# GpSimd's two additions of the output projection's first product, put behind the powers of the layer norms

## The chip, the cores and the metric

The kernel runs on one core of a Trainium2 chip. The metric is the device time of one execution in microseconds (us): before the change the median of six runs is 3116.72 us (3115.21 to 3117.72). The engines of the core work side by side, each through its own list of instructions in a fixed order: TensorE (PE, with its weight loads shown as PEld), VectorE (DVE), ScalarE (ACT), GpSimd (POOL), and SyncE (SP), which here issues the DMAs. An instruction that needs another engine's result waits for a semaphore, and everything behind it on its own engine waits too.

## The reference

For each of 64 batch elements (256 nodes, 512 features) two layers with residual and layer norm are computed in float32:

```python
x = layernorm(x + deg*(x @ Wi.T + b) + adj @ (x @ Wj.T))       # layer 0, a graph layer
q, k, v = (x @ W.T + b  for the three weights)                 # layer 1: attention, 8 heads of 64
attn = softmax(where(adj == 0, -inf, q @ k.T / 8))
x = layernorm(x + (attn @ v) @ Wo.T + bo)
```

`layernorm` subtracts the row's mean and divides by the root of its variance plus 1e-5.

## The kernel before

**Pairs of elements.** The loop at line 982 takes two batch elements per turn `g` (b1 and b2); 32 pairs make the whole, and 31 of them go through the loop. In the turn for pair `g` the attention of pair `g` is computed, and woven into it layer 0 of pair `g+1`, then the output projection of `g` and the projections q, k and v of `g+1`. A turn takes 95.97 us in the trace (the start of the same instruction in successive turns: 1010.83 and 1106.78 us).

**Seven products in place of eight.** Every product with a 512 by 512 weight is made of 2 by 2 blocks by a Strassen-Winograd scheme: seven block products (`pair_steps`, line 646, `block_product`, line 636; eight matmuls each). The left factors are the blocks A11, A12 (of b1), A21, A22 (of b2) and four sums S1 to S4 of them (`left_steps`, line 476, on DVE). For the output projection the blocks lie in `aoT`, which holds the attention's output, and the sums in `oS`. Each product is accumulated in a PSUM bank (tag `mm`, three banks) and then taken out by a `use` function. The order in which the seven run is that of `second_late`: A11, A12, A22, S2, S1, S3, S4.

**The output projection, `o_steps` (line 733).** Its results are added in place to `xh`, which holds the residual. `use1` copies the first product (A11) out of PSUM to a tile `u1` with ACT (line 743), and then GpSimd adds `u1` to one block of b1 (line 746, 128x512) and to both halves of b2 (line 747, 128x1024). The other `use` functions add on DVE (line 740).

**Attention's division.** The sums of the exponentials of a pair of heads come out of four matmuls (`den`); DVE inverts them (line 882), GpSimd adds the inverses to a running total (line 883), DMAs spread them over the partitions (`spread`, line 890), and `multiply` (line 841) multiplies a block of `aoT` by `spread` on GpSimd (line 844). The last division of a turn, `divide_two(g, w + 1)`, concerns block A22 of `aoT`. Its `multiply` therefore has to be over before the sums S1 to S4 are made and before A22 is used by the third product of the output projection.

**The layer norm.** `norm_stats` (line 451) takes mean and variance of 128 rows on DVE, adds 1e-5 (`ve`, line 457), keeps the negated mean (`below`, line 459), and GpSimd raises `ve` to the power -0.5 (`rstd`, line 461). `norm_apply` (line 464) then does two ACT instructions (`shift`, line 466, and `xh`, line 467). In layer 0, `neighbours` multiplies by the graph on TensorE, `take(1)` and `take(0)` add the result to `xh` (line 575) and call `norm_stats`, `give(1)` and `give(0)` call `norm_apply`, and `send_h` writes the rows to DRAM (line 599), from where they come back for a transposition.

**What sets the order.** A planner puts the instructions of each engine in a fixed order when the kernel is built. It goes by its own estimate of when each is ready. `in_order` pins an instruction behind the instruction that the program text issued just before it on the same engine; a pinned one may not overtake that, and an instruction that isn't pinned may be placed earlier. All matmuls are pinned, so TensorE follows the text. `multiply`, `add_bias` and `add_output_bias` on GpSimd are pinned, lines 461, 746 and 747 are not. In the trace of before, GpSimd runs lines 746 and 747 ahead of the two powers.

The place of the change is the end of a turn (lines 1007 to 1010). TensorE's list there is, after the den matmuls of `divide_two`: the first product of the output projection `o[0]` (A11), `neighbours`, `q[0]`, `o[1]` (A12), `k[0]`, `q[1]`, `k[1]`, and then `o[2:6]`, which begin with A22 and S2. `k[1]` accumulates in the bank of `k[0]`, and so it has to wait until ACT has copied `k[0]` out of it (line 711, through `biased`, with the bias `bk`). The copies of q and k are not pinned. The ACT instructions of the norms, lines 466 and 467, are.

The weights' factors come by DMA from SyncE, `next_factor` (line 445), eight tiles ahead.

Of the kernel before, what the change touches and what calls it, by code (L numbers as in the profile page):

```python
# [12 lines left out]
ALU = mybir.AluOpType  # L13
# [3 lines left out]
P = 128  # L17
# [207 lines left out]
def unshifted_path(ctx, tc, flag, x, adj, wiT, wjT, b0, wqT, bq, wkT, bk, wvT, bv, woT, bo, out):  # L225
# [16 lines left out]
    nc = tc.nc  # L242
    B, N, D = x.shape
    NT = N // P
# [5 lines left out]
    H = D // 2  # L250
# [31 lines left out]
    def in_order(ins):  # L282

        tc.keep_in_program_order(ins)
# [44 lines left out]
    mhalf = const.tile([P, 1], F32, name="mhalf")  # L329
# [118 lines left out]
        return f  # L448


    def norm_stats(t, order=anywhere):
        st = small.tile([P, 6], F32, tag="st", name="st")
        order(nc.vector.bn_stats(st, t))
        mv = small.tile([P, 2], F32, tag="mv", name="mv")
        nc.vector.bn_aggr(mv, st)
        ve = small.tile([P, 1], F32, tag="ve", name="ve")
        nc.vector.tensor_scalar(ve, mv[:, 1:2], EPS, None, ALU.add)
        below = small.tile([P, 1], F32, tag="below", name="below")
        order(nc.vector.tensor_scalar(below, mv[:, 0:1], -1.0, None, ALU.mult))  # L459
        rstd = small.tile([P, 1], F32, tag="rstd", name="rstd")  # L460
        nc.gpsimd.tensor_tensor(rstd, ve, mhalf, ALU.pow)  # L461
        return below, rstd

    def norm_apply(t, below, rstd, order=anywhere):
# [37 lines left out]
    def l0_steps(b):  # L502
        banks, k = {}, {}

        def product(name, left, n, first):
            if first:
                banks[name] = bank("po")
            for c in range(2):
                matmul(banks[name], left[:, c, :], w0[:, n, c, :], start=(first and c == 0),
                                 stop=(c == 1), skip_group_check=True)  # L510

        def raw(t, h):
            return xT[b][:, 2 * h:2 * h + 2, t * P:(t + 1) * P]

        def keeper(name):
            k[name] = p3.tile([P, D], F32, tag="lu", name=name)
            return k[name]

        def add_scaled(t, src):
            nc.vector.scalar_tensor_tensor(xh[b][:, t, :], src, deg[:, t:t + 1], xh[b][:, t, :],  # L520
                                           ALU.mult, ALU.add)

        def split(t):
            nc.scalar.copy(k["hi"][:, t, :], k["mj"][:, t, :])
            nc.gpsimd.tensor_tensor(k["lo"][:, t, :], k["mj"][:, t, :], k["hi"][:, t, :].bitcast(F32),
                                    ALU.subtract)

        def step1():
            product("x", raw(0, 0), B11, True)
            nc.scalar.copy(keeper("u1"), banks["x"])  # L530

        def step2():
            product("w", raw(1, 1), T4, True)
            add_scaled(1, banks["w"])

        def step3():
            product("x", raw(0, 1), B21, False)
            add_scaled(0, banks["x"])

        def step4():  # L540
            product("y", xS[b]["S2"], T2, True)
            nc.vector.tensor_add(keeper("u2"), banks["y"], k["u1"])

        def step5():
            product("z", xS[b]["S1"], T1, True)
            k["mj"] = p1.tile([P, NT, D], F32, tag="mj", name="mj")
            nc.scalar.copy(k["mj"][:, 1, :], banks["z"])  # L547

        def step6():
            product("y", xS[b]["S3"], T3, False)  # L550
            nc.vector.tensor_add(keeper("u3"), banks["y"], k["u1"])
            nc.gpsimd.tensor_tensor(k["mj"][:, 1, :], k["mj"][:, 1, :], k["u3"], ALU.add)

            k["hi"] = p1.tile([P, NT, D], F32R, tag="hi", name="hi")
            k["lo"] = p1.tile([P, NT, D], F32R, tag="lo", name="lo")
            split(1)
            add_scaled(1, k["u3"])

        def step7():
            product("z", xS[b]["S4"], B22, False)  # L560
            nc.vector.tensor_add(k["mj"][:, 0, :], banks["z"], k["u2"])
            split(0)

        stats = {}

        def neighbours():
            k["pa"] = score_banks("pa")
            for i in (1, 0):
                for n, (j, part) in enumerate((j, part) for j in (1, 0) for part in ("hi", "lo")):
                    matmul(k["pa"][:, i, :], graph[:, j, i * P:(i + 1) * P], k[part][:, j, :],  # L570
                           start=(n == 0), stop=(n == 2 * NT - 1))

        def take(t):
            r = xh[b][:, t, :]
            in_order(nc.vector.tensor_add(r, k["pa"][:, t, :], r))
            stats[t] = norm_stats(r, in_order)

        def give(t):
            norm_apply(xh[b][:, t, :], *stats[t], in_order)


        return [step1, step2, step3, step4, step5, step6, step7, neighbours, lambda: take(1), lambda: take(0),
                lambda: give(1), lambda: send_h(b, 1), lambda: give(0), lambda: send_h(b, 0)]

# [83 lines left out]
    def second_late(steps):  # L668
        return [steps[0], steps[2], steps[1], *steps[3:]]
# [63 lines left out]
    def o_steps(g):  # L733
        b1, b2 = NB * g, NB * g + 1

        def place(i, j):
            return xh[NB * g + i][:, :, j * H:(j + 1) * H]

        def add_to(dst, src):
            nc.vector.tensor_add(dst, src, dst)  # L740

        def use1(bank, k, new):
            nc.scalar.copy(new("u1"), bank["x"])

            o = xh[b2].rearrange("p t (j o) -> p t j o", j=2)
            nc.gpsimd.tensor_tensor(place(0, 1), place(0, 1), k["u1"], ALU.add)
            nc.gpsimd.tensor_tensor(o, o, k["u1"].unsqueeze(2).to_broadcast([P, NT, 2, H]), ALU.add)

        def use2(bank, k, new):
            add_to(place(1, 0), bank["w"])  # L750

        def use3(bank, k, new):
            add_to(place(0, 0), bank["x"])

        def use4(bank, k, new):
            add_to(place(0, 1), bank["y"])

        def use5(bank, k, new):
            add_to(place(1, 1), bank["z"])

        def use6(bank, k, new):
            o = xh[b2].rearrange("p t (j o) -> p t j o", j=2)
            add_to(o, bank["y"].unsqueeze(2).to_broadcast([P, NT, 2, H]))

        def use7(bank, k, new):
            add_to(place(0, 1), bank["z"])

        steps = pair_steps(lambda: oS[g], False, (use1, use2, use3, use4, use5, use6, use7))
        return second_late(steps)

    def finish_steps(g):

# [136 lines left out]
    def run(steps):  # L909
        for s in steps:  # L910
            s()
# [7 lines left out]
    for g in range(-1, NG - 1):  # L919
        o, q, k, v = (order_of(name) for name in ("wo", "wq", "wk", "wv"))  # L920
# [18 lines left out]
    p, q = l0_steps(0), l0_steps(1)  # L939
# [18 lines left out]
    o = second_late(qk_steps(0, qT, "qT", bq_sb, bqd, True))  # L958
# [23 lines left out]
    for g in range(NG - 1):  # L982
        load_x(NB * (g + 2))
        load_x(NB * (g + 2) + 1)
        work = layer0(g + 1)
        run(work[0])
        for w in range(2, NB * NC, 2):
            values(g, w - 2)
            values(g, w - 1)
            multiply()  # L990
            divide_two(g, w - 1)
            scores(g, w)()
            if w == 4:
                run(work[2])
            later = scores(g, w + 1)
            later()
            run(work[w // 2 if w < 4 else w // 2 + 1])
        w = NB * NC - 2
        values(g, w)
        values(g, w + 1)  # L1000
        multiply()
        o = o_steps(g)
        q = second_late(qk_steps(g + 1, qT, "qT", bq_sb, bqd))
        k = second_late(qk_steps(g + 1, kT, "kT", bk_sb, bkd, True))
        v = second_late(v_steps(g + 1, True))
        neighbours, take1, take0, give1, send1, give0, send0 = work[SLOTS + 1]
        divide_two(g, w + 1)
        run([o[0], neighbours, take1, take0, q[0], give1, send1, o[1], give0, send0, multiply,
             *left_steps(oS[g], in_order), k[0], q[1], k[1]])
        run(o[2:6] + work[SLOTS + 2] + [v[0], o[6], v[1]])  # L1010
        end = finish_steps(g)
        k = with_output_bias(g + 1, k)[2:]
        run(q[2:5] + end[:1] + q[5:6] + end[1:2] + q[6:7] + end[2:3] + k[:1] + end[3:4] + k[1:] + end[4:] + v[2:3])
        turn_x(NB * (g + 2))
        sum_x(NB * (g + 2))
        if g + 2 < NG:
            add_bias(NB * (g + 2))
        run(v[3:5])
        run([scores(g + 1, 0), scores(g + 1, 1)])
        run(v[5:])  # L1020
# [93 lines left out]
```

## Time and profile before

| | |
|---|---|
| median of six runs | 3116.72 us |
| profiled execution, time | 3118.53 us |
| profiled execution, span from the first to the last instruction | 3116.7 us |
| granted TensorE clock, mean | 0.999 |
| PE busy | 3073.6 us (99%), 14598 matmuls |
| DVE busy | 2149.0 us (69%) |
| POOL busy | 1521.0 us (49%) |
| ACT busy | 1008.2 us (32%) |
| line 746 on POOL, 128x512 | 31 times, 1271 ns each |
| line 747 on POOL, 128x1024 | 31 times, 2359 ns each |
| line 461 on POOL, 128x1 | 256 times, 553 ns each |
| line 844 on POOL, 128x512 | 127 times, 1280 ns each |

Times in the trace are counted from the first instruction. A row of the timeline gives the start, the duration, the engine, the line, the operation, the tiles written and read, and how many instructions in a row were merged; in brackets stands how long the engine had been idle before it, and what ended that. "Busy" isn't the same as working at full rate: matmuls are pipelined, and the starts of matmuls that follow each other say more than their durations. All matmuls carry line 290, which is the helper that issues them, so they are told apart by their tiles: `st<-factor,aoT` and `st<-factor,oS` are the output projection, `st<-hT,factor` are q and k.

### The profile page before, as it was taken

How to read it: one execution, taken by the hardware profiler on the slowest of the kernel's cores; microseconds unless marked ns; L12 is line 12 of the kernel's file. 1: busy time of each engine (PE TensorE's matmuls, PEld its weight loads, DVE VectorE, ACT ScalarE, POOL GpSimd, SP SyncE). 2: the span in 40 equal slices, each digit the busy share in tenths (PEclk: the TensorE clock that was granted, in tenths of full speed). 3: DMA queues.
4: the chain of work that ended last, by engine and by line, in shares of the span. 5: the costliest groups of instructions: out<-in, count | busy, mean ns of one | idle time of the engine just before them, and what ended most of it. 6: DMA issues, size and time to landing. Idle time of an engine off the chain costs nothing. (4 is left out here: it accounts for less than half of the span.)

```text
span 3116.7 us, 42777 instructions
## 1 busy us (share of the span) xinstructions
PE 3073.6 (99%) x14598; PEld 2118.5 (68%) x14598; DVE 2149.0 (69%) x3234; ACT 1008.2 (32%) x1925; POOL 1521.0 (49%) x1255
## 2 busy tenths in 40 slices
PE   7999999999999999999999999999999999999998
PEld 4667766677666777666776667766677766677665
DVE  6766676766677666676667676667766667767665
ACT  2332333323333333333233333333333333323332
POOL 2544545544545445464454544455544546445453
PEclk9999999999999999999999999999999999999999
DMA  7355534455444554445553445544455444555333
GB/s 247 122 149 157 166 118 133 131 157 164 141 123 125 156 167 148 119 129 153 158 164 117 126 142 157 165 136 125 127 154 169 141 123 128 154 162 162 115 109 99
DMA packets 410395, 447.28 MB, mean 144 GB/s; under 512 B 40896, under 2 KB 300224, under 8 KB 409792
## 3 DMA queue, kind: packets, MB, share of 16 engines
q1 hardware_dynamic: 410176, 444.50, 47.7%
q8 instruction: 120, 1.97, 0.3%
q14 instruction: 99, 0.81, 0.1%
HBM read 340.79 MB, written 70.25 MB: 132 GB/s over the span
## 5 line engine op out<-in xcount | busy, mean ns | idle before, releaser
L461 POOL TENSOR_TENSOR rstd<-ve,mhalf 128x1 f32<-128x1 f32 x256 | 140.5, 553 | 722.3 <-DVE below L459 722.3
L812 POOL TENSOR_TENSOR pk<-pe 128x512 f32<-128x512 f32 x256 | 322.3, 1275 | 340.7 <-ACT pe L809 340.7
L290 PE MATMUL po<-w,xS 128*128 128x512 f32 x1024 | 470.5, 602 | 6.1 <-ACT mj L547 5.6
L290 PE MATMUL st<-hS,factor 128*128 128x256 f32 x2048 | 452.7, 379 | 1.2 <-DVE u L685 1.2
L290 PEld LDWEIGHTS st<-hS,factor 128*128 128x128 f32 x2048 | 388.2, 190 | 55.3 <-DVE u L685 1.6
L809 ACT ACTIVATE pe<-pe 128x1024 f32<-128x1024 f32 x256 | 270.8, 1058 | 379.2 <-DVE pe L805 379.2
L290 PE MATMUL st<-hT,factor 128*128 128x256 f32 x1536 | 360.7, 381 | 9.0 <-ACT u L711 8.3
L290 PE MATMUL po<-w,xT 128*128 128x512 f32 x768 | 354.4, 604 | 14.6 <-DVE xS L479 9.3
L290 PEld LDWEIGHTS po<-w,xS 128*128 128x128 f32 x1024 | 187.0, 190 | 252.8 <-issue 191.4
L290 PEld LDWEIGHTS st<-hT,factor 128*128 128x128 f32 x1536 | 289.0, 190 | 61.5 <-ACT u L711 20.7
L805 DVE TENSOR_TENSOR pe<-ps,maskT 128x1024 f32<-128x1024 f32 x256 | 297.7, 1194 | 35.2 <-PE ps L290 35.2
L882 DVE RECIPROCAL rden<-den 128x256 f32<-128x256 f32 x127 | 222.8, 1754 | 73.9 <-PE den L290 68.4
L290 PEld LDWEIGHTS po<-w,xT 128*128 128x128 f32 x768 | 144.4, 192 | 182.9 <-issue 163.6
L290 PE MATMUL ps<-qT,kT 64*128 64x256 f32 x2048 | 264.9, 392 | 0.0
L883 POOL TENSOR_TENSOR rtot<-rtot,rden 128x256 f32<-128x256 f32 x127 | 92.7, 730 | 330.4 <-DVE rden L882 330.4
L290 PE MATMUL pav<-pe,v_sb 128*64 128x256 f32 x2048 | 250.1, 386 | 1.9 <-ACT pe L809 1.8
L740 DVE TENSOR_TENSOR xh<-st,xh 128x512 f32<-128x512 f32 x186 | 144.5, 777 | 147.8 <-PE st L290 147.7
L290 PEld LDWEIGHTS pav<-pe,v_sb 128*64 128x64 f32 x2048 | 135.2, 136 | 154.1 <-issue 72.0
L290 PEld LDWEIGHTS ps<-qT,kT 64*128 64x128 f32 x2048 | 184.3, 186 | 78.2 <-issue 51.3
L290 PE MATMUL st<-factor,hS 128*128 128x256 f32 x1024 | 234.8, 382 | 0.0
L290 PE MATMUL st<-factor,oS 128*128 128x256 f32 x992 | 224.2, 379 | 0.0
L290 PEld LDWEIGHTS st<-factor,hS 128*128 128x128 f32 x1024 | 191.9, 190 | 35.4 <-issue 10.6
(115 smaller groups left out, 4657.8 us busy)
## 6 DMA issues: line engine op xcount, KB each, us to landing
xB<-in_x_dram SPq DMA_DIRECT2D x256, 128.0 KB, 3.7
xh<-in_x_dram SPq DMA_DIRECT2D x64, 512.0 KB, 4.1
factor<-wq SPq DMA_DIRECT2D x128, 256.0 KB, 4.4
factor<-wk SPq DMA_DIRECT2D x128, 256.0 KB, 2.6
factor<-wv SPq DMA_DIRECT2D x128, 256.0 KB, 2.6
spread<-rden SPq DMA_DIRECT2D x1016, 32.0 KB, 1.9
factor<-wo SPq DMA_DIRECT2D x124, 256.0 KB, 3.0
h_cols<-xh SPq DMA_DIRECT2D x124, 256.0 KB, 2.5
```

The source lines that it names most:

```text
L290: in_order(nc.tensor.matmul(*args, **kw))
L461: nc.gpsimd.tensor_tensor(rstd, ve, mhalf, ALU.pow)
L740: nc.vector.tensor_add(dst, src, dst)
L805: nc.vector.tensor_add(pe.rearrange("p j t q -> p j (t q)"), ps.rearrange("p j t q -> p j (t q)"), maskT.rearrange("p t q -> p (t q)").uns ...
L809: in_order(nc.scalar.activation(flat, flat, AF.Exp, scale=QSCALE, accum_out=etot[:, NB * g + i, pr:pr + 1]))
L812: nc.gpsimd.tensor_tensor(pk, pe[:, :, 0, :], pe[:, :, 1, :], ALU.add)
L882: nc.vector.reciprocal(rden, den)
L883: nc.gpsimd.tensor_tensor(rtot, rtot, rden, ALU.add)
```

## The change

`norm_stats` gets a second argument, with which the power on GpSimd can be pinned; `take` in layer 0 gives it, so the powers of layer 0's norms are pinned behind what the text issued before them on GpSimd. The powers of the last norms (`finish_steps`) stay free. In `o_steps` the two GpSimd additions leave `use1` and become a step of their own, `add_first`, the eighth of the list (`o[7]`), and they are pinned. In the run of a turn's end that step stands behind `take0`. As `multiply` is pinned too, GpSimd's order at that place is fixed by the text: power, power, line 746, line 747, and then the multiplication of line 844.

```diff
-    def norm_stats(t, order=anywhere):
+    def norm_stats(t, order=anywhere, power_order=anywhere):
...
-        nc.gpsimd.tensor_tensor(rstd, ve, mhalf, ALU.pow)
+        power_order(nc.gpsimd.tensor_tensor(rstd, ve, mhalf, ALU.pow))
         return below, rstd
...
         def take(t):
             r = xh[b][:, t, :]
             in_order(nc.vector.tensor_add(r, k["pa"][:, t, :], r))
-            stats[t] = norm_stats(r, in_order)
+            stats[t] = norm_stats(r, in_order, in_order)
...
+        kept = []
+
         def use1(bank, k, new):
             nc.scalar.copy(new("u1"), bank["x"])
+            kept.append(k["u1"])
+
+        def add_first():
 
             o = xh[b2].rearrange("p t (j o) -> p t j o", j=2)
-            nc.gpsimd.tensor_tensor(place(0, 1), place(0, 1), k["u1"], ALU.add)
-            nc.gpsimd.tensor_tensor(o, o, k["u1"].unsqueeze(2).to_broadcast([P, NT, 2, H]), ALU.add)
+            in_order(nc.gpsimd.tensor_tensor(place(0, 1), place(0, 1), kept[0], ALU.add))
+            in_order(nc.gpsimd.tensor_tensor(o, o, kept[0].unsqueeze(2).to_broadcast([P, NT, 2, H]), ALU.add))
...
-        return second_late(steps)
+        return second_late(steps) + [add_first]
...
-        run([o[0], neighbours, take1, take0, q[0], give1, send1, o[1], give0, send0, multiply,
+        run([o[0], neighbours, take1, take0, o[7], q[0], give1, send1, o[1], give0, send0, multiply,
              *left_steps(oS[g], in_order), k[0], q[1], k[1]])
```

## The prediction

> **What bounds the kernel now.** First the page's busy shares, then the waits of TensorE, then the timeline of one turn's end (the turn whose `neighbours` start at 1103.26 us).
>
> ```profile
> PE 3073.6 (99%) x14598; PEld 2118.5 (68%) x14598; DVE 2149.0 (69%) x3234; ACT 1008.2 (32%) x1925; POOL 1521.0 (49%) x1255
> ```
>
> TensorE is busy for 99% of the span, GpSimd for half of it. So time that GpSimd or ACT saves is worth nothing in itself: only what makes a matmul or a weight load start later or earlier counts. The waits of the weight loads in the 30 turns that lie whole between 143 and 3023 us:
>
> ```profile
> PEld po L290 <- ACT mj L547: 30.3, 30, 1.0
> PEld pav L290 <- DVE xS L478: 22.7, 30, 0.8
> PEld st L290 <- ACT u L711: 20.1, 30, 0.7
> ```
>
> The third row is the one at the place of the change: once a turn a load for `st` waits for ACT's copy of line 711. No row names GpSimd's `aoT` of line 844, so the last multiplication is in time today. The timeline shows why both are so:
>
> ```profile
> 1105.55 1.27 POOL L746 TENSOR_TENSOR xh<-xh,u 128x512 f32<-128x512 f32 x1
> ...
> 1106.78 2.36 POOL L747 TENSOR_TENSOR xh<-xh,u 128x1024 f32<-128x1024 f32 x1
> ...
> 1107.19 0.15 DVE L457 TENSOR_SCALAR ve<-mv 128x1 f32<-128x1 f32 x1
> ...
> 1108.78 3.62 PE L290 MATMUL st<-hT,factor 128*128 128x256 f32 x16
> 1108.99 0.15 DVE L457 TENSOR_SCALAR ve<-mv 128x1 f32<-128x1 f32 x1
> ...
> 1109.09 1.07 POOL L461 TENSOR_TENSOR rstd<-ve,mhalf 128x1 f32<-128x1 f32 x2
> ...
> 1110.63 1.27 POOL L844 TENSOR_TENSOR aoT<-aoT,spread 128x512 f32<-128x512 f32 x1 [0.46 <-DMA spread<-rden]
> ...
> 1111.04 0.81 ACT L467 ACTIVATE xh<-xh,shift,rstd 128x512 f32<-128x512 f32 x1
> ...
> 1111.76 0.82 ACT L711 ACTIVATE u<-st,bk 128x256 f32<-128x256 f32 x2
> ...
> 1111.93 0.69 DVE L477 TENSOR_TENSOR oS<-aoT 128x512 f32<-128x512 f32 x1 [2.13 <-POOL aoT L844]
> ...
> 1112.63 1.59 PEld L290 LDWEIGHTS st<-hT,factor 128*128 128x128 f32 x8 [0.64 <-ACT u L711]
> 1112.63 1.99 PE L290 MATMUL st<-hT,factor 128*128 128x256 f32 x8 [0.24 <-ACT u L711]
> ...
> 1114.25 1.70 PEld L290 LDWEIGHTS st<-factor,aoT 128*128 128x128 f32 x8
> 1114.46 1.89 PE L290 MATMUL st<-factor,aoT 128*128 128x256 f32 x8
> ...
> 1115.98 5.15 PEld L290 LDWEIGHTS st<-factor,oS 128*128 128x128 f32 x24
> 1116.19 5.34 PE L290 MATMUL st<-factor,oS 128*128 128x256 f32 x24
> ```
>
> To be read: the first power's `ve` is ready at 1107.34, but GpSimd is still adding until 1109.14. The powers run late, the four ACT instructions of the norms follow them, the copy of `k[0]` (`u<-st,bk`) stands behind these on ACT and ends at 1112.58, and `k[1]` starts at 1112.63. The eight matmuls between 1114.46 and 1116.19 give the undisturbed step, 1.73 / 8 = 0.216 us. Sixteen of them from 1108.78 (`k[0]`, `q[1]`) end the step at 1112.24: `k[1]` lost 0.39. Its own eight take 1.83 instead of 1.73, so a stopped stream loses another 0.10 on restarting. Together 0.49 per turn here. The multiplication ended at 1111.90, long before the load at 1114.25 that needs it.
>
> **The change part by part.** All of it lies on GpSimd's list; nothing is computed more or less, and no DMA is issued from that list.
>
> *The powers of line 461 move ahead of lines 746 and 747.* The first power runs at 1107.34 + 0.08 = 1107.42 (0.08 is what lies between the end of `ve`, 1131.82 + 0.15, and a power that found GpSimd idle, 1132.05). The second, whose `ve` ends at 1109.14, at 1109.22. So both norms' ACT work comes earlier: `shift` at 1109.22 + 0.55 + 0.04 = 1109.81 (0.04 from the rows of now, power's end 1109.64 and `shift` at 1109.68), `xh` 0.33 later, and the copy of `k[0]` 0.72 after that (1110.01 to 1109.68, 1111.76 to 1111.04), so at 1110.86, ending at 1111.68. `k[1]`'s load is wanted at 1112.24 - 0.21 = 1112.03. Its wait goes, and A22's product could start at 1114.46 - 0.49 = 1113.97, its weight load at 1113.76.
>
> *Lines 746 and 747 move behind the second power.* GpSimd has nothing else to do between the first power (over at 1107.97) and the second: 1.25 us that the additions would have filled stay empty. Line 746 starts 0.52 after the second power (the step from a lone power at 1138.48 to the next instruction at 1138.99 is 0.51): 1109.74. Line 747 follows after 1.23 (1105.55 to 1106.78): 1110.97. Its successor after 2.31 (1106.78 to 1109.09): 1113.28. Who waits for the additions: DVE's additions of A22's product to the same `xh`, not before 1116.4. That costs nothing.
>
> *`multiply` (line 844) is queued behind them, and this is the price.* It starts at 1113.28 rather than 1110.63 and ends at 1114.55. `spread` lands before: in the latest turn of all the multiplication starts 9.11 after `neighbours` began, and the new start is 1113.28 - 1103.26 = 10.02 after it. Who waits for line 844: A22's weight load, and DVE's line 477. A result passes to PE in 0.05 (1112.58 to 1112.63), so the load and the first matmul stand at 1114.60, which is 0.84 after the 1113.76 at which the load was wanted. S2's product comes 1.83 later, with the restart's loss: 1116.43 rather than 1116.19.
>
> *The sums S1 to S4 on DVE*: line 477 at 1114.55 + 0.03 = 1114.58, S2 (line 478) 0.73 later and over after 0.69, at 1116.00. S2's load is wanted at 1116.43 - 0.21 = 1116.22. It's hidden by the eight matmuls of A22, with 0.17 to spare. If that cover goes, the excess is lost in each turn.
>
> *The rest.* Layer 0's other powers, in the middle of a turn and before the loop, already stand in the text's order in the trace: nothing. SyncE's `h_cols` DMA of line 599 waits for ACT's `xh` and is issued up to 1.7 earlier; `hB` isn't read before 1122.7, so nothing. `u1` is held 4.2 longer in a ring of four whose next turn comes with k's sums: nothing.
>
> *The sum.* This turn ends 0.24 later. It is one with a small wait of now; over the turns S2's product begins 12.93 to 13.00 after `neighbours`, 12.95 in most, here 12.93. Against 12.95 it is 1116.43 - 1103.26 - 12.95 = 0.22. Thirty-one turns make 6.8 us: the span goes from 3116.7 to 3123.5, the profiled execution from 3118.53 to 3125.3, and the median, 1.8 below that execution, from 3116.72 to **3123.5 us** (+0.22%). The gain on `k[1]` isn't subtracted again: with A22's load gated at 1114.60, it doesn't matter whether `k[1]` started at 1112.24 or 1112.63. One wait replaces another that is longer by 0.22.
>
> *Bounds of what the trace doesn't show.* (1) A pinned addition behind a power: 0.51 by the row used; 0.3 more if it has a gap like the ten rows of line 844 with idle time put down to issue (3.0 us in ten). I take 0.51, the same sequence of kinds. (2) The additions' durations in the new place: GpSimd's line 552 takes 1.28 alone at 26.25 us and 1.78 at 1098.40, beside DVE's line 520 with two operands in SBUF. Beside lines 746 and 747 there will be only line 740, with one operand in PSUM, and then an idle DVE; 1.27 and 2.36 hold for 31 turns of now, beside line 575 of the same kind. I take 0; the other end is 0.4 x 3.6 = 1.4 per turn, which nothing near suggests. (3) Hand-over to PE: 0.03 to 0.05. (4) The additions could be at most 0.01 quicker (the shortest is 1266 ns). A gain from these terms is excluded past 0.02 per turn.
>
> *A rule weighed.* Line 747 takes 2.36 us for 1024 elements and line 746 1.27 for 512. The Trainium skill (GPSIMD Engine Reference, section 3.1) gives GpSimd's two-operand addition some 2.6 cycles per element at 1.2 GHz, as an estimate from it 2.22 and 1.11 us without the dispatch. By these the three instructions would take 4.44 in place of the 4.81 of the rows, the multiplication would end 0.37 earlier, and the turn would be 0.15 shorter than now, 4.7 us in all. The rows decide. The same page (section 1) names contention with DVE instructions of two SBUF operands; by that the moved additions have no such neighbour.
>
> **The rivals.** A difference of less than 0.2% (6.2 us) can't be told from no change here.
>
> *A, faster: the multiplication is in time after all, and only `k[1]`'s wait goes.* For it: that wait is in every turn. Then 0.49 to 0.53 per turn is won (most turns have a load's wait of 0.64 to 0.66 in place of this turn's 0.62), 16 us: 3100.5. It asks for an end of line 844 at 1113.71, 0.84 earlier than worked out; it breaks even at 1114.33, 0.22 earlier. Against it: the second `ve` waits for two 128x512 passes of DVE that nothing here shortens, and all behind it is one engine's list.
>
> *B, clearly slower: S2 comes late.* If the planner puts one DVE instruction of 0.69 between the multiplication and S2, or the sums start 0.3 to 0.5 late, the 0.17 to spare are gone and 0.5 per turn is lost on top: 0.5 x 31 = 16 us, 3139. Less than that, a gap on GpSimd as in bound (1), gives 0.5 per turn in all, 3133. For it: the planner's order of free DVE instructions may shift. Against it: line 477 is pinned and DVE is idle for 2.13 in front of it.
>
> *C, no change.* The planner or the chip gives GpSimd's chain back 0.2: 3117. For it: the margin is small. Against it: bound (4).
>
> **How the numbers follow.** The case worked out: 0.62, with its own range 3121.5 to 3126 (0.16 to 0.30 per turn). A: 0.13. B in both forms: 0.17. C: 0.08. The range leaves out A and the dear half of B and reaches from C to the gap on GpSimd: 3116.5 to 3133.5. The threshold lies at 3122.95, inside the likeliest case, of which I count 0.38 of its 0.62 as slower and 0.24 as the same. Slower: 0.38 + 0.17 = 0.55. Same: 0.24 + 0.08 = 0.32. Faster: 0.13.
>
> **What would show it.** In the changed profile: two powers 1.8 apart, lines 746, 747 and 844 back to back behind the second; no row of `st` waiting for ACT's line 711, but one of `st` waiting for GpSimd's `aoT`, 31 times, some 0.87 each; A22's matmuls 11.3 after `neighbours` and S2's 13.17; a turn of 96.19 us. Wrong it would be through a `ve` that comes at another time, additions of another length, a DVE instruction ahead of S2, or a new order elsewhere in the turn.

## The result and the profile after

The changed kernel takes 3124.01 us (median of 20 runs, 3121.75 to 3125.36), the kernel before 3116.11 us (median of 40): a ratio of 1.0022, with a 95% interval of 1.0016 to 1.0028. It is slower, by 5.0 to 8.7 us. The forecast was 3123.5 us against 3116.72, which is 1.0022 too.

The busy shares tell nothing, as is to be expected where only an order changes:

```profile
PE 3073.2 (98%) x14598; PEld 2121.7 (68%) x14598; DVE 2145.8 (69%) x3234; ACT 1012.1 (32%) x1925; POOL 1521.7 (49%) x1255
```

The waits of TensorE's weight loads in the changed kernel, in the same stretch from 143 to 3023 us as before (total us, times, longest us; the rows left out name `issue` or are shorter):

```profile
...
PEld po L290 <- ACT mj L547: 30.3, 30, 1.0
PEld st L290 <- POOL aoT L849: 26.4, 30, 0.9
PEld pav L290 <- DVE xS L478: 22.7, 30, 0.8
...
```

Lines 466 to 740 carry the same numbers in both kernels; line 844 of before is 849 now, and lines 746 and 747 are 751 and 752. Of the three rows of before the outer two stand as they were. The row `st <- ACT u L711` with its 20.1 us is gone, and in its place `st` waits for GpSimd's `aoT`, 26.4 us in 30 turns. The timeline of the turn whose `neighbours` start at 1104.74 us:

```profile
1108.90 0.55 POOL L461 TENSOR_TENSOR rstd<-ve,mhalf 128x1 f32<-128x1 f32 x1 [1.81 <-DVE below L459]
...
1110.25 5.34 PE L290 MATMUL st<-hT,factor 128*128 128x256 f32 x24
1110.46 0.15 DVE L457 TENSOR_SCALAR ve<-mv 128x1 f32<-128x1 f32 x1
...
1110.69 0.55 POOL L461 TENSOR_TENSOR rstd<-ve,mhalf 128x1 f32<-128x1 f32 x1 [1.24 <-DVE below L459]
1111.21 1.28 POOL L751 TENSOR_TENSOR xh<-xh,u 128x512 f32<-128x512 f32 x1
...
1112.33 0.82 ACT L711 ACTIVATE u<-st,bk 128x256 f32<-128x256 f32 x2
1112.44 2.35 POOL L752 TENSOR_TENSOR xh<-xh,u 128x1024 f32<-128x1024 f32 x1
...
1114.75 1.26 POOL L849 TENSOR_TENSOR aoT<-aoT,spread 128x512 f32<-128x512 f32 x1
...
1116.05 0.69 DVE L477 TENSOR_TENSOR oS<-aoT 128x512 f32<-128x512 f32 x1 [4.78 <-POOL aoT L849]
1116.07 1.59 PEld L290 LDWEIGHTS st<-factor,aoT 128*128 128x128 f32 x8 [0.88 <-POOL aoT L849]
1116.07 2.00 PE L290 MATMUL st<-factor,aoT 128*128 128x256 f32 x8 [0.48 <-POOL aoT L849]
1116.77 0.69 DVE L478 TENSOR_TENSOR oS<-oS,aoT 128x512 f32<-128x512 f32 x1
...
1117.90 2.32 PE L290 MATMUL st<-factor,oS 128*128 128x256 f32 x10
```

The first good sign is on TensorE: `k[0]`, `q[1]` and `k[1]` run as 24 matmuls in one piece, where before they broke after 16. The copy of `k[0]` ends at 1113.15 and no one waits for it. The new wait is on GpSimd: 1.24 us idle in front of the second power, then power, additions and multiplication without a gap, and TensorE's load stands 0.88 us until the multiplication is over at 1116.01.

Nothing but GpSimd's list is in another order in the trace, and there only the two powers and the two additions have changed places, once in each of 31 turns. The change has two parts, the pin on the powers and the additions' new place; no run takes them apart, so what each does by itself isn't shown.

### The profile page after: what moved, and what is told of

It is laid out like the page before. It is cut to its first block, busy times and chain, and to the rows that moved or that the text cites. A ratio compares the mean times of both kernels' runs of the same rounds, so it can differ in the third digit from the quotient of the medians.

```text
span 3122.2 us, 42777 instructions
## 1 busy us (share of the span) xinstructions
PE 3073.2 (98%) x14598; PEld 2121.7 (68%) x14598; DVE 2145.8 (69%) x3234; ACT 1012.1 (32%) x1925; POOL 1521.7 (49%) x1255
## 5 line engine op out<-in xcount | busy, mean ns | idle before, releaser
L290 PE MATMUL st<-hT,factor 128*128 128x256 f32 x1536 | 352.4, 379 | 0.7 <-ACT hT L622 0.7
L467 ACT ACTIVATE xh<-xh,shift,rstd 128x512 f32<-128x512 f32 x256 | 208.5, 814 | 8.6
```

The source lines that it names most:

```text
L290: in_order(nc.tensor.matmul(*args, **kw))
L467: order(nc.scalar.activation(t, t, AF.Identity, bias=shift, scale=rstd))
```

## The experiments

Two theories stood against the one of the prediction (GpSimd's chain after the second power gates A22's load): that the kernel loses because the additions to `xh` come late (rival 1), and that GpSimd's order has nothing to do with it (rival 2). The "turn" in what follows is the start of `neighbours` in the last of the 31 turns less that in the first, divided by 30. The next three columns are medians over the turns, in us after `neighbours` began. Each ratio is to runs of before taken beside that kernel (medians 3115.95 to 3117.40 us; 3116.11 is that beside the changed kernel).

| kernel | time, us | ratio to before (95%) | turn, us | multiplication over | A22's first matmul | S2's first matmul |
|---|---|---|---|---|---|---|
| before | 3116.11 | 1 | 95.98 | 8.64 | 11.22 | 12.95 |
| changed | 3124.01 | 1.0022 (1.0016 to 1.0028) | 96.19 | 11.27 | 11.32 | 13.15 |
| e2, small addition between the powers | 3099.17 | 0.9942 (0.9929 to 0.9956) | 95.45 | 10.06 | 10.69 | 12.42 |
| e7, e2 and a pass of 128x256 | 3107.54 | 0.9970 (0.9960 to 0.9981) | 95.67 | 10.75 | 10.81 | 12.64 |
| e3, changed and a pass of 128x512 | 3157.22 | 1.0129 (1.0114 to 1.0145) | 97.30 | 12.39 | 12.44 | 14.27 |
| e1, multiplication before the additions | 3133.44 | 1.0058 (1.0045 to 1.0072) | 96.52 | 8.65 | 10.69 | 13.28 |
| e4, S3 before S2 | 3130.60 | 1.0041 (1.0027 to 1.0055) | 96.42 | 11.28 | 11.34 | 13.31 |

**e2: the gap filled.** The small addition goes where GpSimd stood idle, between the powers:

```diff
-        run([o[0], neighbours, take1, take0, o[7], q[0], give1, send1, o[1], give0, send0, multiply,
+        run([o[0], neighbours, take1, o[7], take0, o[8], q[0], give1, send1, o[1], give0, send0, multiply,
```

(`add_first` is split for it: `o[7]` is the addition to b1, `o[8]` that to b2.)

> The small addition (128x512) goes between the two powers, where the changed kernel leaves GpSimd idle for 1.24 us; the large one stays behind the second power. Theory: the second power is not delayed, the multiplication ends 1.23 earlier, at 10.05 after neighbours, before the 10.43 that would still be in time, so both waits are gone: 3099.7 us. Rival 1 (late additions): the additions end 1.23 earlier than in the changed kernel but later than before; between 3116 and 3122 us. Rival 2: 3124 us.

It took 3099.17 us. The timeline of this kernel (line 749 is the small addition, 753 the large one, 850 the multiplication):

```profile
1099.52 0.55 POOL L461 TENSOR_TENSOR rstd<-ve,mhalf 128x1 f32<-128x1 f32 x1 [1.80 <-DVE below L459]
1100.04 1.27 POOL L749 TENSOR_TENSOR xh<-xh,u 128x512 f32<-128x512 f32 x1
...
1101.31 0.55 POOL L461 TENSOR_TENSOR rstd<-ve,mhalf 128x1 f32<-128x1 f32 x1
1101.83 2.36 POOL L753 TENSOR_TENSOR xh<-xh,u 128x1024 f32<-128x1024 f32 x1
...
1104.14 1.28 POOL L850 TENSOR_TENSOR aoT<-aoT,spread 128x512 f32<-128x512 f32 x1
...
1105.84 1.70 PEld L290 LDWEIGHTS st<-factor,aoT 128*128 128x128 f32 x8
1106.05 1.89 PE L290 MATMUL st<-factor,aoT 128*128 128x256 f32 x8
```

The second power starts 1.79 after the first, as in the changed kernel, so the addition cost it nothing. The multiplication is over at 1105.42, the load runs at 1105.84 and waits for no one. The turn is 0.53 shorter than before, the price of `k[1]`'s wait as the prediction had it. Neither the wait for ACT that the kernel before has nor the wait for GpSimd that the changed one has is left, and all it took is one instruction in another place on GpSimd's list. This is the fastest kernel of the study; it beats before and changed.

**e3: the chain made longer.** One more addition, on the tile `u1` that no one reads any more, in front of the multiplication:

```diff
             in_order(nc.gpsimd.tensor_tensor(o, o, kept[0].unsqueeze(2).to_broadcast([P, NT, 2, H]), ALU.add))
+            in_order(nc.gpsimd.tensor_tensor(kept[0], kept[0], kept[0], ALU.add))
```

> The changed kernel with one more GpSimd addition of 128x512, on a tile that nobody reads any more, between the two additions and the multiplication. Theory: the multiplication and all that waits for it move by the pass's step of 1.23 us in each turn: 31 x 1.23 = 38 us, 3162 us, and A22's load waits 2.1 instead of 0.88 us. Rival 1 (late additions): the additions are where they were; 3124 us. Rival 2: 3124 us, or 3126 if GpSimd's work as such costs something.

The multiplication ended 1.12 later than in the changed kernel (12.39 and 11.27), and the turn grew by 1.11 (97.30 and 96.19): one for one. A22's load waits 2.0 instead of 0.88:

```profile
PEld st L290 <- POOL aoT L850: 59.9, 30, 2.0
```

The pass itself is cheaper than I had priced it, 1042 ns by its group's mean, with one tile as both operands, so the 38 us became 33 (3157.22 less 3124.01). The additions to `xh` stand where they stood; rivals 1 and 2 fall here.

**e7: where the price begins.** e2 with a pass of half that size behind the large addition (`o[8]`):

```diff
+            in_order(nc.gpsimd.tensor_tensor(kept[0][:, 0, :], kept[0][:, 0, :], kept[0][:, 0, :], ALU.add))
```

> The kernel with the small addition between the powers, and one more GpSimd addition of 128x256 (on a tile that nobody reads any more) behind the large one, so that the multiplication ends some 0.70 later. It looks for the point from which the price begins. Theory: the multiplication ends at 10.75 after neighbours; the load that is wanted at 10.48 starts at 10.80, 0.32 late, and with 0.10 for the restart the turn is 0.42 longer than without any wait: 3099.7 + 31 x 0.42 = 3112.7 us. Rival 1 (late additions): the same time as without the extra pass. Rival 2: 3124 us.

The multiplication ended at 10.75, as expected, but the turn grew by 0.22 over e2 and not by 0.42. The waits of the weight loads in this kernel:

```profile
PEld st L290 <- POOL aoT L851: 10.6, 30, 0.4
```

The wait is there, 0.35 each. My sum had a fault: it counted the load's delay of 0.32, but an undisturbed load runs 0.21 ahead of its matmul, and in a stopped stream both start together (1116.07 above). What counts is the matmul's start, 10.81 in place of 10.69, and 0.10 for the restart. Here the load came 0.33 late (10.81 for 10.48) and its matmul 0.12. From this I infer that a load that is up to 0.21 late delays no matmul; no run has a lateness that small, so whether it would still cost a restart isn't shown.

**e1: the multiplication first.** Had the multiplication been the whole story, this would have been as good as e2:

```diff
-        run([o[0], neighbours, take1, take0, o[7], q[0], give1, send1, o[1], give0, send0, multiply,
+        run([o[0], neighbours, take1, take0, q[0], give1, send1, o[1], give0, send0, multiply, o[7],
```

> GpSimd's order at a turn's end becomes power, power, multiplication (line 844 of before), and then the two additions, all pinned. Theory (the multiplication at the end of GpSimd's chain gates A22's weight load): the multiplication is over 7.8 to 10.4 us after neighbours began, before the 10.48 at which the load is wanted, and ACT's copy of the first k product stays early; neither wait is left. Per turn 0.53 less than before: 31 x 0.53 = 16.4 us, 3099.7 us. Rival 1 (the changed kernel loses because the additions to xh come late, and DVE's additions or the norms wait for them): the additions end later than in the changed kernel, some 11.9 after neighbours instead of 10.0, so 3124 us or more. Rival 2 (GpSimd's order doesn't matter, the changed kernel loses through something that the timeline doesn't tie to it): 3124 us.

It was the slowest but one in the table, 3133.44 us, as rival 1 would have it. A22's load was in time, at 10.69 the matmul was where it is in e2. The timeline shows the place of the loss:

```profile
1113.69 1.27 POOL L849 TENSOR_TENSOR aoT<-aoT,spread 128x512 f32<-128x512 f32 x1 [0.86 <-DMA spread<-rden]
...
1114.92 1.28 POOL L751 TENSOR_TENSOR xh<-xh,u 128x512 f32<-128x512 f32 x1
1115.00 1.75 DVE L477 TENSOR_TENSOR oS<-aoT 128x512 f32<-128x512 f32 x1 [2.14 <-POOL aoT L849]
...
1116.15 2.81 POOL L752 TENSOR_TENSOR xh<-xh,u 128x1024 f32<-128x1024 f32 x1
1116.78 2.72 DVE L478 TENSOR_TENSOR oS<-oS,aoT 128x512 f32<-128x512 f32 x1
...
1119.57 5.05 PEld L290 LDWEIGHTS st<-factor,oS 128*128 128x128 f32 x24 [1.07 <-issue]
```

S1 takes 1.75 us on DVE and S2 2.72, where each takes 0.69 in the other kernels. S2 is over at 1119.50, and its product's load starts 0.07 after that, having stood for 1.07 (the trace puts this down to `issue`, and not to S2 by name; before, changed and e2 have no such wait). The durations tell how: line 477 begins 0.08 after GpSimd's small addition and ends 0.55 after it; the large addition is put down as starting at 1116.15, takes 0.45 longer than its 2.36, and ends at 1118.96; line 478 ends 0.54 after that. Each seems to hold something that the next one needs from start to end. By their tiles no data ties the additions to the sums.

**e9: the additions left out.** The same kernel without GpSimd's two additions, in order to see whether they slow the sums:

> The kernel with the multiplication directly behind the second power, with GpSimd's two additions of the first product left out altogether (the output lacks that product in three of its four blocks). It asks why DVE's sums S1 and S2 took 1.75 and 2.72 us there and not 0.69 each. Theory (GpSimd's additions beside them slow these DVE instructions, which have two operands in SBUF): without the additions both take 0.69 again, S2 is over at 10.1 after neighbours, no wait is left at that place, and the turn is 95.45 us long: 3099.7 us. Rival (the sums are slow because they follow the multiplication so early, or wait for something else): they stay at 1.75 and 2.72 us, and the time at 3133 us.

```diff
-... give0, send0, multiply, o[7],
+... give0, send0, multiply,
```

It took 3100.54 us (ratio 0.9947, 0.9930 to 0.9963), with a turn of 95.45, the same as e2. DVE's group of S2, in e1 and then in e9 (31 instructions: total busy us, mean ns):

```profile
L478 DVE TENSOR_TENSOR oS<-oS,aoT 128x512 f32<-128x512 f32 x31 | 84.4, 2723 | 1.1
```

```profile
L478 DVE TENSOR_TENSOR oS<-oS,aoT 128x512 f32<-128x512 f32 x31 | 21.4, 692 | 1.1
```

So it is the additions beside them that make S1 and S2 slow, not their early start. Rival 1 is no better off, although e9 takes away late additions as well: S1 and S2 don't read `xh`, and no wait of DVE for the additions appears in e1's trace. The additions harm by running beside DVE, not by being late. The Trainium skill (SBUF — State Buffer, section "SBUF: two separate sides") says that GpSimd and a DVE instruction with two SBUF inputs use one pair of ports, which goes to the one that starts first for its whole length. The rows of e1 agree with that in every step, with 2.72 us for an instruction of 0.69. The kernel before has the other case, in which DVE starts first:

```profile
1098.29 0.75 DVE L520 SCALAR_TENSOR_TENSOR xh<-u,deg,xh 128x512 f32<-128x512 f32 x1
1098.40 1.78 POOL L552 TENSOR_TENSOR mj<-mj,u 128x512 f32<-128x512 f32 x1 [1.48 <-DVE u L551]
```

There DVE keeps its 0.75 and GpSimd's addition takes 1.78 in place of the 1.28 that it takes alone.

**e4: the cover of S2.** The prediction had left S2 0.17 us of room in the changed kernel.

```diff
-             *left_steps(oS[g], in_order), k[0], q[1], k[1]])
+             *[left_steps(oS[g], in_order)[i] for i in (0, 2, 1, 3)], k[0], q[1], k[1]])
```

> The changed kernel with DVE's sum S3 made before S2. It tests the cover of 0.17 us that the prediction gave to S2. Theory: S2 comes 0.6 later, 0.43 beyond its cover, and TensorE waits a second time in each turn; with some 0.1 for the restart 0.43 to 0.53 per turn: 13 to 16 us, 3137 to 3140 us. If S2 has more cover than that, or isn't waited for: 3124 us.

S2 came 0.49 later (its end 13.21 in place of 12.72 after `neighbours`), not 0.6, S2's first matmul 0.16 later, and the turn is 0.23 longer. One turn's rows:

```profile
1118.96 0.68 DVE L478 TENSOR_TENSOR oS<-oS,aoT 128x512 f32<-128x512 f32 x1
...
1119.71 1.38 PEld L290 LDWEIGHTS st<-factor,oS 128*128 128x128 f32 x7 [0.35 <-issue]
```

This second wait of 0.35 stands in each of the 31 turns, 0.07 past the end of S2, so the cover is as small as worked out. The price was put too high by the 0.1 that S2 came earlier than expected, and by the fault that e7 shows: the 0.21 between load and matmul is cover as well.

**e8: A22's product later.** This asked TensorE to do other work while the multiplication runs:

```diff
-        run(o[2:6] + work[SLOTS + 2] + [v[0], o[6], v[1]])
+        run(v[:2] + o[2:6] + work[SLOTS + 2] + [o[6]])
```

> The changed kernel's order on GpSimd, but TensorE does the first two products of v (16 matmuls, 3.45 us) before the four of the output projection that begin with A22, instead of among and after them; the factors' DMAs are issued in that order too. Theory: A22's load is wanted only 13.9 after neighbours, the multiplication is over at 11.28, so the wait for it is gone while GpSimd's list is untouched: 3099.7 us, up to 5 us more if the products that now come later wait for a bank. Rival 1 (late additions): the additions are where they were, 3124 us. Rival 2: 3124 us.

It took 3191.19 us (1.0238, 1.0224 to 1.0252), which none had expected, and it can't be read as a verdict on the theories. A22's first matmul stands at 15.09 with the multiplication over at 11.28, and no load waits for GpSimd. But my edit brought waits of its own. TensorE's waits, in total us:

```profile
PE st L290 <- issue: 49.7, 31, 1.6
PE st L290 <- ACT u L729: 20.9, 31, 0.7
```

The second row is `v[1]`, which accumulates in the bank of `v[0]` and now follows it at once, before ACT has copied the bank; the first is q's product with A22 of the new pair. It needs a transposition (line 485) that DVE makes behind the additions of the output projection, and starts 0.07 after it (1151.30, and 1149.18 + 2.05). In the changed kernel two of v's products stand in front of that product of q, and one of the output projection between `v[0]` and `v[1]`; these had been the cover. What a well-placed A22 would give wasn't tried.

## Why the prediction was right

- *The wait of `k[1]` goes.* Right: the row is gone, the 24 matmuls run in one piece. Its worth, given as 0.49 to 0.53 per turn under rival A, is 0.53 by e2.
- *The additions behind the second power, and the empty gap of 1.25.* Right: powers at 4.15 and 5.95 after `neighbours` (worked out: 4.16 and 5.96), GpSimd idle for 1.24 in front of the second. e2 shows that with this gap filled no wait is left at that place.
- *The multiplication ends at 11.29 after `neighbours`, A22's matmul at 11.34.* Right: 11.27 and 11.32 in the median turn. The other estimate that the prediction weighed, from 2.6 cycles per element (0.37 earlier, 4.7 us faster than before), doesn't come true; the rows of before were the better guide.
- *S2 follows with 0.17 to spare.* Right in size; e4 takes the cover away. That the matmul itself has another 0.21 wasn't seen, so rival B's price for a late S2 was too high by that. The forecast doesn't rest on it, as S2 was in time.
- *No new neighbour for the additions on DVE* (bound 2). Right: 1275 and 2355 ns in the new place. e1 shows what the bound was about: had the multiplication been put ahead of them, DVE's sums would have been the neighbours, at 1.07 us per turn (e1 beside e2).
- *The sum.* 0.22 per turn was worked out, 0.21 measured, 31 turns make 6.4 us in place of 6.8. The medians are 7.9 apart, the interval of the ratio runs from 5.0 to 8.7 us and holds both. That the forecast of 3123.5 lies only 0.5 us from the measured 3124.01 is in part luck: the median of before was 0.6 lower this time, and the difference 1.1 larger than forecast.
- *Rival A* (3100.5 us) isn't what the change does, but it is what e2 does: its condition, an end of the multiplication 0.84 earlier, is met by filling the gap (1.20 earlier), and its price of 16 us fits 31 turns of 0.53. One reading under it is off by 0.02: the load's wait in the turn shown is 0.64 by its row, not 0.62, and 0.66 to 0.68 in most turns; the difference between them stands.

## What to carry to other kernels

On an engine in strict order, moving an instruction behind another that isn't ready yet moves everything that is queued there, and the price is read at the last thing in that queue which the bounding engine needs; here the step that was freed (0.53) was worth less than the one delayed (0.74). Look for idle time in front of the instruction that is to go first, and put there what fits into it: 1.24 us of idle time took an addition of 1.27 and turned a loss of 0.2% into a gain of 0.6%. Before two engines are made to work at the same time, see whether they hinder one another, and which of them starts first: an addition of 0.69 us on DVE took 2.72 beside one on GpSimd that had begun before it.

## What the runs showed of the hardware that was not expected

- A DVE addition with two operands in SBUF (128x512) took 1.74 and 2.72 us beside GpSimd's additions of 128x512 and 128x1024, in place of 0.69; the large GpSimd addition took 2.80 in place of 2.36, the small one 1.27 as always. There DVE lost more, but it isn't always the loser: in the kernel before, where line 520 on DVE began 0.11 ahead of line 552 on GpSimd, DVE lost nothing and GpSimd 0.50 (rows 1098.29 and 1098.40).
- A GpSimd addition of 128x512 with the same tile as both operands took 1042 ns, with two tiles 1275.
- A weight load that waited starts at the same time as its matmul (within 0.04 us in the rows of this case), where an undisturbed one runs 0.21 ahead, and the step to the next matmul is 0.32 in place of 0.216. So in e7 a load that came 0.33 late delayed its matmul by only 0.12, and the stop cost 0.10 more.
- The first turn's `neighbours` began between 140.3 and 143.4 us in the profiled executions of the nine kernels, which do the same work up to there. So a difference of 2 us between two profiled spans can come from there; the turn's length is the better measure, and e2 and e9, where nothing waits at that place, agree in it (95.45 us).
